# A graph layer with convolutions by frequency: gate weights summed one per batch, statistics in a row, weight transforms ahead of the first convolution, another order of tiles in the last phase, z behind n at the end

## The chip, the cores and the metric

One core of one Trainium2 chip. The metric is the device time of one execution in microseconds (us). The core has TensorE (PE; its weight loads PEld), VectorE (DVE), ScalarE (ACT), GpSimd (POOL) and SyncE (SP); SPq, ACTq and POOLq mark DMA issues on an engine's queue. A tile is a named buffer on the chip, PSUM the memory that TensorE writes to. A transfer is issued by one instruction and has landed when its data is there. The granted clock is the share of its full clock that TensorE had.

## The reference, cut to what matters

```python
h = relu(layernorm(x))                         # x: (32, 512, 256), 32 batches
# one layer on h; its result is added to x
c = relu(bn1(conv1(h)))                        # 1 tap
c = bn2(conv2(c))                              # 17 taps
x_conv = relu(c + h)
s = h @ w_se.T + b_se                          # 3 columns
A = exp(-dist(s, s)) * adj                     # (32, 512, 512), adj is 0 or 1
x_nmp = A @ relu(h @ w_msg.T + b_msg)
gi = concat(x_conv, x_nmp) @ w_ih.T ; gh = h @ w_hh.T
r = sigmoid(gi_r + gh_r) ; z = sigmoid(gi_z + gh_z)
n = tanh(gi_n + r * gh_n)
return x + (1 - z) * n + z * h
```

## The kernel before

The 17 tap convolution is a product over frequencies, the gates use a seven-product form of the 2 x 2 block product. So the program runs through these stages:

1. First stage, batches 0 to 15: layer norm, transpose, first convolution, transform to frequencies (tile `xf`), and beside it the transform of the convolution's weights (`pw`).
2. First nodes stage, batches 0 to 15: messages, adjacency, sums of messages, and the products over the frequencies (`py`).
3. Second stage, batches 16 to 31, without weight transforms. GpSimd forms the combined gate weights (`combine_weights`) in it.
4. Second nodes stage, batches 16 to 31.
5. Last phase, 16 pairs of batches: inverse transform (`inverse`), gates r, z, n, blend, transposes back, store.

The parts that the change and the argument touch:

```python
def statistics(b):
    ...
    for c in range(NC):                                   # NC = 4
        nc.vector.bn_stats(stats[:, c, :], X[b][:, c, :])
        nc.vector.bn_aggr(mv[:, c, :], stats[:, c, :])
    nc.vector.tensor_scalar(rstd, mv[:, :, 1], LN_EPS, None, op0=ALU.add)
    nc.gpsimd.tensor_tensor(rstd, rstd, minus_half[:, :NC], op=ALU.pow)
...
def load_adj(b):                                          # one buffer
    ADJ[b] = pools["nodes"].tile([P, N // 32, P], FP, tag="adj", name=f"adj_{b}", bufs=1)
    rows = adj[b].rearrange("(j r) (g m) -> g r j m", r=32, g=4)
    for g in range(4):
        nc.sync.dma_start(ADJ[b][32 * g : 32 * (g + 1)], rows[g])      # pieces of 128 floats
...
def combine_weights(k):                                   # called in three batches of stage 3
    w = pools["sums"].tile([P, DC, G], FP, tag="wraw", ...)
    nc.sync.dma_start(w, src...)
    ...
    for dst, a in ((Q1, a11), (Q2, a12), (Q4, a22)):
        nc.gpsimd.tensor_copy(t[:, dst], a)
    nc.gpsimd.tensor_tensor(t[:, Q5], a21, a22, op=ALU.add)
    ...                                                   # three more sums, then one store
...
def load_pair(p, queue=nc.sync):
    NP[p] = pools["ops"].tile([P, 7, N], FP, tag="np", ...)
    HP[p] = pools["ops"].tile([P, 8, N], FP, tag="hp", ...)
    ...                                                   # yt tiles in the loop behind them
...
with phase("late"), phase("sw"), phase("ops", bufs=2), phase("work"), tc.manual_schedule():
    sw = pools["sw"].tile([P, K3, 7, 3, P], FP, name="sw")
    load_pair(0, nc.gpsimd)
    load_combined(sw, 0, 2)                               # on GpSimd's queue, 4.1 MB in all
    load_combined(sw, 2, 7)
    inverse(0)
    ...
        gates_rz(p, terms, between)
        ...
        gate_n(p, terms, not more)                        # with blend and store of the last pair
```

## Time and profile before

| | before |
|---|---|
| median of 3 runs | 1972.78 us (1970.61 to 1972.83) |
| span of the profiled run | 1971.5 us |
| first stage, to the first `pm` matmul | 181.2 us |
| first nodes stage, to the first `phT` of batch 16 | 309.1 us |
| second stage, to the first `pm` of the second nodes stage | 138.0 us |
| second nodes stage, to its last `pm`, and from there to the inverse | 280.5 + 29.9 us |
| inverse of the first pair, to the first gate matmul | 15.2 us |
| rest of the last phase | 1017.7 us |

The stages are read off TensorE's timeline: each ends where the first matmul of the next one starts. The prediction below shows the page and the waits. Two places that it did not look at closely also belong here, so they stand here. The first is one batch of the first stage on VectorE (start in us, duration, engine, line, operation; in brackets the idle time before and what ended it):

```profile
65.66 0.69 DVE L221 COPY wst<-pw 80x512 f32<-80x512 f32 x1 [1.64 <-PE pw L214]
66.27 0.41 DVE L234 BATCH_NORM_STATS2 stats<-x 128x6 f32<-128x256 f32 x1
66.72 0.18 DVE L235 BATCH_NORM_AGGREGATE mv<-stats 128x2 f32<-128x6 f32 x1
...
68.52 0.17 DVE L238 TENSOR_SCALAR rstd<-mv 128x4 f32<-128x4 f32 x1
...
72.49 1.27 DVE L221 COPY wst<-pw 80x512 f32<-80x512 f32 x2
```

Four such pairs follow each other, so from the first statistic to the instruction that adds epsilon pass 2.25 us. Behind it come the additions and copies out of PSUM that TensorE needs. VectorE waits for TensorE only once in the batch, 1.64 us, and TensorE waits in the same batch for the copies out of PSUM:

```profile
73.75 1.89 PE L214 MATMUL pw<-w2p,taps 17*80 17x512 f32 x8 [0.28 <-ACT wst L223]
```

So here the two engines hand work to each other in a loop, and a share of busy time (in 45.8 to 75.6 us VectorE 79%, TensorE 97%) does not tell which of them sets the pace. TensorE's busy time holds waiting, too: eight such `pw` matmuls take 1.10 us at 70.00 and 1.89 us here.

The second place is the end of the second nodes stage, the last adjacency loads and their reader:

```profile
917.80 1.38 SPq L330 DMA_DIRECT2D adj<-in_adj_dram  x3
...
921.65 0.35 SPq L405 DMA_DIRECT2D nd<-nmp  x1
...
928.38 2.06 DVE L390 STREAM_TRANSPOSE at<-adj 128x512 f32<-128x512 f32 x2
```

The fourth load follows the store at 922.04 (0.43 us). The reader has no bracket: it did not wait. The loads of the last two batches took 3.2 to 5.6 us from issue to landing.

### The profile page before, as it was taken

Reading aid. Unit: us, or ns where it says so; the run is one execution under the profiler, and the core shown is the slowest. Engines: PE = TensorE matmul, PEld = TensorE weight load, DVE = VectorE, ACT = ScalarE, POOL = GpSimd, SP = SyncE. Lnnn points to the kernel's source line nnn. Section 1 sums busy time; section 2 is a strip of 40 time slices with the busy share of each in tenths; the row PEclk is TensorE's granted clock in tenths of the full one; section 3 lists DMA queues with packets and bytes.
Section 4 is the critical chain, followed back from the end, with each engine's and each line's share of the span. In section 5 each row is a group of like instructions: output and inputs, shape, how many; then the busy total and the mean of one; then the engine's idle time right before and its main releaser. Section 6 shows DMA issues by size and latency. Waiting matters only on the chain.

```text
span 1971.5 us, 21287 instructions
## 1 busy us (share of the span) xinstructions
PE 1916.8 (97%) x7328; PEld 1185.1 (60%) x7328; DVE 1131.3 (57%) x2191; ACT 545.2 (28%) x930; POOL 570.3 (29%) x564
## 2 busy tenths in 40 slices
PE   7999999999888999999899999999999999999997
PEld 5667676766777767775555545555455554555453
DVE  7776666665775665656155455544555355544555
ACT  3545332332234333332122212222122221222121
POOL 2231333333332344432613322132212322133211
PEclk9999999999899999999899999999999999999998
DMA  8997987776554788785812443134421443134401
GB/s 209 287 262 221 250 240 233 232 215 208 180 175 144 215 245 260 228 240 153 267 46 80 126 126 97 42 113 125 126 61 65 126 126 112 41 98 126 126 12 53
DMA packets 237055, 309.89 MB, mean 157 GB/s; under 512 B 14339, under 2 KB 187331, under 8 KB 236563
## 3 DMA queue, kind: packets, MB, share of 16 engines
q1 hardware_dynamic: 217715, 251.48, 44.3%
q0 software_dynamic: 7008, 25.17, 4.6%
q10 hardware_dynamic: 12224, 31.86, 4.6%
q8 instruction: 59, 0.97, 0.2%
q14 instruction: 49, 0.40, 0.1%
HBM read 201.57 MB, written 106.89 MB: 156 GB/s over the span
## 4 chain that ended last, share of the span: by engine, by line
PE 88%; DVE 5%; DMA 3%; issue 2%; POOL 1%; ACT 1%; SPq 0%; POOLq 0%; DVEq 0%; ACTq 0%
PE pg L490 29%; PE pn L490 14%; PE pn L399 11%; PE py L317 10%; PE pm L350 6%; PE pc L479 5%; PE pc L269 3%; PE px L284 2%; PE pd L385 2%; PE po L619 2%; PE pw L214 1%; DVE stats L234 1%; DMA wd<-wst 1%; PE phT L256 1%; DMA sw<-ws 1%
## 5 line engine op out<-in xcount | busy, mean ns | idle before, releaser
L490 PE MATMUL pg<-hp,sw 128*128 128x512 f32 x448 | 229.9, 595 | 0.3 <-DMA sw<-ws 0.3
L490 PE MATMUL pg<-np,sw 128*128 128x512 f32 x448 | 229.3, 593 | 0.0
L490 PE MATMUL pg<-cp,sw 128*128 128x512 f32 x448 | 228.7, 592 | 0.0
L399 PE MATMUL pn<-A,msg 128*128 128x512 f32 x512 | 225.5, 593 | 0.3 <-DVE A L391 0.3
L468 POOL TENSOR_TENSOR hp<-hp 128x512 f32<-128x512 f32 x64 | 80.6, 1270 | 460.1 <-DMA hp<-hd 393.2
L399 PEld LDWEIGHTS pn<-A,msg 128*128 128x128 f32 x512 | 96.9, 190 | 111.6 <-issue 108.2
L503 ACT ACTIVATE rz<-rz,brz 128x512 f32<-128x512 f32 x96 | 69.3, 722 | 298.7 <-DVE rz L507 298.7
L309 POOL TENSOR_TENSOR both<-xf 128x256 f32<-128x256 f32 x78 | 61.0, 782 | 309.6 <-PE py L317 273.7
L317 PE MATMUL py<-wt,both 128*128 128x256 f32 x624 | 150.4, 384 | 0.0
L490 PEld LDWEIGHTS pg<-np,sw 128*128 128x128 f32 x448 | 85.4, 191 | 107.7 <-issue 106.4
L490 PEld LDWEIGHTS pg<-cp,sw 128*128 128x128 f32 x448 | 85.2, 190 | 107.5 <-issue 107.2
L390 DVE STREAM_TRANSPOSE at<-adj 128x512 f32<-128x512 f32 x128 | 136.1, 1098 | 10.8 <-DMA adj<-in_adj_dram 7.8
L468 POOL TENSOR_TENSOR cp<-cp 128x512 f32<-128x512 f32 x64 | 80.5, 1268 | 210.6 <-ACT cp L484 209.3
L317 PEld LDWEIGHTS py<-wt,both 128*128 128x128 f32 x624 | 114.2, 190 | 43.9 <-issue 27.0
L490 PEld LDWEIGHTS pg<-hp,sw 128*128 128x128 f32 x448 | 82.9, 191 | 92.8 <-issue 89.5
L312 POOL TENSOR_TENSOR wsum<-wt 128x512 f32<-128x512 f32 x78 | 106.0, 1361 | 78.9 <-DMA wt<-wd 66.6
L269 PE MATMUL pc<-w,hT 128*128 128x256 f32 x512 | 127.6, 406 | 0.6 <-DVE hT L257 0.6
L479 PEld LDWEIGHTS pc<-back,yt 120*128 120x128 f32 x1024 | 119.5, 195 | 12.5 <-issue 7.7
L350 PE MATMUL pm<-wmsg,hT 128*128 128x259 f32 x512 | 125.6, 398 | 0.0
L479 PE MATMUL pc<-back,yt 120*128 120x80 f32 (+1 forms) x1024 | 119.2, 278 | 4.6 <-DMA yt<-yd 4.6
L350 PEld LDWEIGHTS pm<-wmsg,hT 128*128 128x128 f32 x512 | 122.3, 327 | 0.7
L490 PE MATMUL pn<-hp,sw 128*128 128x512 f32 x224 | 115.1, 595 | 0.0
(117 smaller groups left out, 2888.0 us busy)
## 6 DMA issues: line engine op xcount, KB each, us to landing
wt<-wd SPq DMA_DIRECT2D x160, 256.0 KB, 5.5
adj<-in_adj_dram SPq DMA_DIRECT2D x128, 256.0 KB, 5.1
yd<-y ACTq DMA_DIRECT2D x80, 384.0 KB, 5.6
yt<-yd SPq DMA_DIRECT2D x60, 480.0 KB, 9.4
wd<-wst SPq DMA_DIRECT2D x64, 320.0 KB, 5.2
x<-in_x_dram SPq DMA_DIRECT2D x38, 512.0 KB, 5.9
hd<-hT SPq DMA_DIRECT2D x32, 512.0 KB, 3.9
nd<-nmp SPq DMA_DIRECT2D x32, 512.0 KB, 3.2
```

The lines of the kernel that those rows point to most:

```text
L269: nc.tensor.matmul(p[:, j, :], HT[b][:, ic, c * P : (c + 1) * P], w1[:, ic, :], start=(ic == 0), stop=(ic == DC - 1))
L284: nc.tensor.matmul(p[:, j * 2 * L : (j + 1) * 2 * L], H1[b][:, c0 + j, ic * P : (ic + 1) * P], fwd, start=True, stop=True)
L309: nc.gpsimd.tensor_tensor(both[:, 0], re, im, op=ALU.add)
L312: nc.gpsimd.tensor_tensor(wsum, wr, wi, op=ALU.add)
L317: nc.tensor.matmul(dst, v[:, ic, :], w[:, ic, :], start=(ic == 0), stop=(ic == DC - 1))
L350: nc.tensor.matmul(p[:, : D + NS], chunk(HT[b][:, ic, :], c), wmsg[:, ic, :], start=(ic == 0), stop=(ic == DC - 1))
L390: nc.vector.transpose(at.rearrange("p (j k) -> p j k", k=32), ADJ[b].rearrange("p j (q c) -> p c j q", c=NC)[:, mc])
L399: nc.tensor.matmul(p, MSG[b][:, mc, dc * P : (dc + 1) * P], A[b][:, mc, :], start=(mc == 0), stop=(mc == NC - 1))
L468: nc.gpsimd.tensor_tensor(t[:, dst, :], t[:, a, :], t[:, b, :], op=sub)
L479: nc.tensor.matmul(bk[:, t0:t1], YT[p][j * W + w][:, oc * P : (oc + 1) * P], back[:, u0 : u0 + t1 - t0], start=(w == 0), stop=(w == W - 1) ...
L490: nc.tensor.matmul(bk, sw[:, k, q, o, :], terms[k][q], start=(first and i == 0), stop=(i == len(ks) - 1), skip_group_check=True)
L503: nc.scalar.activation(rz[:, g, j, :], src, AF.Sigmoid, bias=brz[:, g : g + 1], scale=1.0)
```

## The change

It means to take seven GpSimd instructions at a time out of the way of GpSimd's other work in the second stage, to shorten the statistics, to load less at the start and make the first weight transforms ahead of the first convolution, to let the first loads of the last phase start early by laying their tiles over memory that is free early, and to end with z, which needs less work behind its last matmul than n. The prediction numbers these five parts: 1 gate weights, 2 statistics, 3 first tiles of the last phase, 4 start, 5 z behind n. The core of the diff:

```diff
-    load_x(1)                                   # at the start
...
             nc.vector.bn_stats(stats[:, c, :], X[b][:, c, :])
+        for c in range(NC):
             nc.vector.bn_aggr(mv[:, c, :], stats[:, c, :])
...
-    def combine_weights(k):
...
+    def combine_weights():
+        steps = []
+        for k, src in enumerate((w_hhT, w_ihT[D:], w_ihT[:D])):
+            w, t = (pools["sums"].tile([P, n, 3, P], FP, tag=f"w{n}", name=f"w{n}_{k}") for n in (4, 7))
+            ...
+            for j in range(4):
+                nc.sync.dma_start(w[:, j], a[:, j // 2, j % 2])
+            ...                                  # four sums, one step each, no copies
+            steps[-1] = partial(self_and_store, steps[-1], k, stores)     # seven stores
...
     def load_pair(p, queue=nc.sync):
+        yt = [pools["ops"].tile([ROWS, W // 2, D], FP, tag="yt", ...) for k in range(4)]
+        HP[p] = pools["ops"].tile([P, 8, N], FP, tag="hp", name=f"hp_{p}")
         NP[p] = pools["ops"].tile([P, 7, N], FP, tag="np", name=f"np_{p}")
-        HP[p] = pools["ops"].tile([P, 8, N], FP, tag="hp", name=f"hp_{p}")
...
         if g == 0:                              # first weight transforms ahead of the first convolution
+            one, two = between(b0)
+            for step in one:
+                step()
             transpose_h(b0)
+            for step in two:
+                step()
...
-            load_taps(gen, 1, nc.sync)          # now loaded in batch 0's turn, on GpSimd's queue
...
-                    if b % 4 == 2 and b // 4 < K3:
-                        combine_weights(b // 4)
-                    return [], []
+                    return combine[b - 2 : b - 1] if b > 1 else [], []
...
+                gates_rz(p, terms, between, [0])                    # last pair: r
+                gate_n(p, terms, True)                              # n
+                gates_rz(p, terms, lambda i: None, [1], then)       # z, with blend and store
```

More of the change, by code (lines that the diff above doesn't have):

```diff
@@ L416, in gnn_layer, with self_and_store @@
     B11, B12, B21, B22 = range(4)
-    def combine_weights(k):
-        src = [w_hhT, w_ihT[D:], w_ihT[:D]][k]
-        w = pools["sums"].tile([P, DC, G], FP, tag="wraw", name=f"wraw_{k}")
-        nc.sync.dma_start(w, src.rearrange("(c p) o -> p c o", p=P))
-        w = w.rearrange("p c (g i o) -> p c g i o", i=2, o=P)
-        a11, a21, a12, a22 = w[:, 0, :, 0], w[:, 0, :, 1], w[:, 1, :, 0], w[:, 1, :, 1]
-        t = pools["sums"].tile([P, 7, 3, P], FP, tag="wsum7", name=f"wsum7_{k}")
-        for dst, a in ((Q1, a11), (Q2, a12), (Q4, a22)):
-            nc.gpsimd.tensor_copy(t[:, dst], a)
-        nc.gpsimd.tensor_tensor(t[:, Q5], a21, a22, op=ALU.add)
-        nc.gpsimd.tensor_tensor(t[:, Q6], t[:, Q5], a11, op=ALU.subtract)
-        nc.gpsimd.tensor_tensor(t[:, Q7], a11, a21, op=ALU.subtract)
-        nc.gpsimd.tensor_tensor(t[:, Q3], a12, t[:, Q6], op=ALU.subtract)
-        nc.sync.dma_start(WS[k], t)
+    def combine_weights():
+        steps = []
+        for k, src in enumerate((w_hhT, w_ihT[D:], w_ihT[:D])):
+            w, t = (pools["sums"].tile([P, n, 3, P], FP, tag=f"w{n}", name=f"w{n}_{k}") for n in (4, 7))
+            a = src.rearrange("(c p) (g i o) -> p c i g o", p=P, i=2, o=P)
+            for j in range(4):
+                nc.sync.dma_start(w[:, j], a[:, j // 2, j % 2])
+            a11, a21, a12, a22 = (w[:, j] for j in range(4))
+            for dst, x1, x2, op in ((Q5, a21, a22, ALU.add), (Q6, t[:, Q5], a11, ALU.subtract),
+                                    (Q7, a11, a21, ALU.subtract), (Q3, a12, t[:, Q6], ALU.subtract)):
+                steps.append(partial(nc.gpsimd.tensor_tensor, t[:, dst], x1, x2, op=op))
+            stores = [(Q1, a11), (Q2, a12), (Q4, a22)] + [(q, t[:, q]) for q in (Q5, Q6, Q7, Q3)]
+            steps[-1] = partial(self_and_store, steps[-1], k, stores)
+        return steps
+    def self_and_store(step, k, stores):
+        step()
+        for q, src in stores:
+            nc.sync.dma_start(WS[k][:, q], src)
     def load_combined(sw, q0, q1):
@@ L437, in load_pair @@
     def load_pair(p, queue=nc.sync):
+        yt = [pools["ops"].tile([ROWS, W // 2, D], FP, tag="yt", name=f"yt_{p}_{k}", bufs=5) for k in range(4)]
+        HP[p] = pools["ops"].tile([P, 8, N], FP, tag="hp", name=f"hp_{p}")
         NP[p] = pools["ops"].tile([P, 7, N], FP, tag="np", name=f"np_{p}")
-        HP[p] = pools["ops"].tile([P, 8, N], FP, tag="hp", name=f"hp_{p}")
         YT[p] = []
@@ L445, in load_pair @@
             for k in range(2):
-                t = pools["ops"].tile([ROWS, W // 2, D], FP, tag="yt", name=f"yt_{b}_{k}", bufs=5)
+                t = yt[2 * j + k]
                 w = w0 + k * (W // 2)
@@ L494, in temp, with gates_rz @@
         return pools["late"].tile([P, N], FP, tag=role, name=f"{role}_{name}", bufs=2)
-    def gates_rz(p, terms, between):
-        RZ[p] = rz = pools["late"].tile([P, 2 * DC, 2, N], FP, tag="rz", name=f"rz_{p}", bufs=1)
+    def gates_rz(p, terms, between, outs=range(2), then=lambda i, j: None):
+        if 0 in outs:
+            RZ[p] = pools["late"].tile([P, 2 * DC, 2, N], FP, tag="rz", name=f"rz_{p}", bufs=1)
+        rz = RZ[p]
         ks = range(K3)
@@ L508, in result @@
             sigmoid(dst, o, i, j)
-        for o in range(2):
+            then(i, j)
+        for o in outs:
             b1[o] = bank(f"pg1_{p}_{o}")
@@ L514, in gates_rz @@
             nc.scalar.copy(p1[o], b1[o])
-        for o in range(2):
+        for o in outs:
             b2[o] = bank(f"pg2_{p}_{o}")
@@ L519, in gates_rz @@
             nc.vector.tensor_add(u2[o], p1[o], b2[o])
-        for o in range(2):
+        for o in outs:
             into(b1[o], Q2, o, ks, terms, False)
             sigmoid(b1[o], o, 0, 0)
+            then(0, 0)
         between(0)
-        for o in range(2):
+        for o in outs:
             into(b2[o], Q7, o, ks, terms, False)
@@ L528, in gates_rz @@
         between(1)
-        for o in range(2):
+        for o in outs:
             b3[o] = bank(f"pg3_{p}_{o}")
@@ L532, in gates_rz @@
             result(b3[o], u3[o], o, 1, 1)
-        for o in range(2):
+        for o in outs:
             into(b2[o], Q4, o, ks, terms, False)
             result(b2[o], p1[o], o, 1, 0)
-        for o in range(2):
+        for o in outs:
             into(b3[o], Q3, o, ks, terms, False)
@@ L563, in closing @@
             nc.scalar.activation(n, n, AF.Tanh, bias=b_in[:, i : i + 1], scale=1.0)
-        def blend(i, j, engine=nc.vector):
-            n, d = nt[:, i, j, :], rz[:, i, j, :]
-            engine.tensor_tensor(d, HP[p][:, 2 * i + j, :], n, op=ALU.subtract)
-            engine.tensor_tensor(d, d, rz[:, DC + i, j, :], op=mul)
-            engine.tensor_tensor(n, n, d, op=add)
         x1 = [bank(f"pn1_{p}_{k}") for k in range(2)]
@@ L598, in gate_n, with blend @@
         closing(x3[1], 0, 1)
-        if last:
-            blend(0, 0, nc.gpsimd)
-            blend(1, 1, nc.gpsimd)
-            blend(1, 0)
-            finish(p, 0)
-            blend(0, 1)
-            finish(p, 1)
-        else:
-            for i, j in ((0, 0), (1, 1), (1, 0), (0, 1)):
-                blend(i, j)
+        for i, j in ((0, 0), (1, 1), (1, 0), (0, 1)):
+            nc.vector.tensor_sub(rz[:, i, j, :], HP[p][:, 2 * i + j, :], nt[:, i, j, :])
+            if not last:
+                blend(p, i, j)
+    def blend(p, i, j):
+        n, d = NT[p][:, i, j, :], RZ[p][:, i, j, :]
+        nc.vector.tensor_mul(d, d, RZ[p][:, DC + i, j, :])
+        nc.vector.tensor_add(n, n, d)
     def finish(p, j):
@@ L638, in first_part @@
         if g == 0:
+            one, two = between(b0)
+            for step in one:
+                step()
             transpose_h(b0)
+            for step in two:
+                step()
         statistics(b0 + 1)
@@ L654, in first_part @@
                 normalise(b + 2)
-            one, two = between(b - b0)
+            one, two = between(b - b0) if b > 0 else ([], [])
             if b > b0:
@@ L681, in gnn_layer @@
             load_taps(gen, 0, nc.sync)
-            load_taps(gen, 1, nc.sync)
             def between(b):
-                if b and b % 2 == 0 and b // 2 + 1 < QI // PI:
+                if b % 2 == 0 and b // 2 + 1 < QI // PI:
                     load_taps(gen, b // 2 + 1)
@@ L737, in gnn_layer @@
             with phase("first", "sums"):
+                combine = combine_weights()
                 def between(b):
-                    if b % 4 == 2 and b // 4 < K3:
-                        combine_weights(b // 4)
-                    return [], []
+                    return combine[b - 2 : b - 1] if b > 1 else [], []
                 xf = freq_tile(1)
@@ L773, in between, with then @@
                         sums(NP[p + 1], False)
-            gates_rz(p, terms, between)
             if more:
+                gates_rz(p, terms, between)
                 inverse(p + 1)
                 sums(CP[p + 1], False)
-            gate_n(p, terms, not more)
+                gate_n(p, terms, False)
+            else:
+                def then(i, j):
+                    blend(p, i, j)
+                    if i != j:
+                        finish(p, j)
+                gates_rz(p, terms, between, [0])
+                gate_n(p, terms, True)
+                gates_rz(p, terms, lambda i: None, [1], then)
 def kernel(**inputs):
```

## The prediction

> **What bounds the kernel now.** I read the page's engine table and slices first, then TensorE's waits, then the timeline at each place where TensorE stands still.
>
> ```profile
> PE 1916.8 (97%) x7328; PEld 1185.1 (60%) x7328; DVE 1131.3 (57%) x2191; ACT 545.2 (28%) x930; POOL 570.3 (29%) x564
> PE   7999999999888999999899999999999999999997
> PEclk9999999999899999999899999999999999999998
> ...
> PE 88%; DVE 5%; DMA 3%; issue 2%; POOL 1%; ACT 1%; SPq 0%; POOLq 0%; DVEq 0%; ACTq 0%
> ```
>
> TensorE is busy 1916.8 of 1971.5 us and is 88% of the chain that ended last. The change alters no matmul, so only the 55 us of idle time and the stretches at a lower granted clock can shrink. The waits tell where those 55 us are:
>
> ```profile
> PE phT L256 <- issue: 12.9, 3, 5.9
> PE po L619 <- DVE nt L570: 9.5, 2, 6.7
> PE row L158 <- DVE diag L157: 9.0, 1, 9.0
> PE pc L479 <- DMA yt<-yd: 4.6, 2, 2.6
> ```
>
> (what waited, total us, times, longest). That is four places: the second convolution stage, the end, the start, and the entry to the last phase. The steady part of the last phase has none. The "issue" label of the first line hides the cause; the timeline of one of its three stalls shows it:
>
> ```profile
> 517.26 0.17 DVE L238 TENSOR_SCALAR rstd<-mv 128x4 f32<-128x4 f32 x1
> 517.60 1.41 POOL L426 COPY wsum<-wraw 128x384 f32<-128x384 f32 x3 [5.49 <-DMA wraw<-in_w_hhT_dram]
> 521.94 0.99 POOL L430 TENSOR_TENSOR wsum<-wraw,wsum 128x384 f32<-128x384 f32 x1
> 523.69 1.05 POOL L239 TENSOR_TENSOR rstd<-rstd,minus_half 128x4 f32<-128x4 f32 x1
> 524.78 1.45 DVE L245 TENSOR_SCALAR x<-x,mv,rstd 128x256 f32<-128x256 f32 x4 [6.15 <-POOL rstd L239]
> 525.29 2.03 PE L256 MATMUL phT<-ident,x 128*128 128x128 f32 x8 [2.25 <-issue]
> 527.00:531.00 4.00, 4.00 (x14) 3.29 (x13) 0.42 (x1) 2.38 (x6) 0.00 (x0) 0.62 0.95 335
> ```
>
> VectorE had the variance at 517.4, but GpSimd raised it to -0.5 only at 523.7, because the seven weight sums stood in its queue. The last line is a window's row (busy of PE, PEld, DVE, ACT, POOL, then the granted clock): after the gap the clock falls to 0.62.
>
> **What the Trainium skill says.** "TensorE: Matmul & The Clock Gate", Part 1 (The HAM clock gate): an idle TensorE drops to half clock and returns after a few us of work. The trace agrees: 4 us at mostly 0.50 after a 2.25 us gap, so a stall costs its gap and about 2 us more. The same page, "Architectural detail", calls the queues of ScalarE, VectorE and GpSimd strict FIFO: the 6.15 us above is such a wait. "DMA: Bandwidth & Descriptors", "Queues, rings and completion order": each DMA engine takes turns between queues packet by packet, so an earlier bulk load slows a later urgent one. This trace has no clean case of it. "SBUF — State Buffer", "Who interferes with whom": a VectorE instruction with two SBUF inputs contends with GpSimd's reads. At the end L558 takes 1.64 us beside a GpSimd blend, against its 0.72 us mean.
>
> **The change part by part.**
>
> *1. Gate weights, one sum per batch.* Transforms of successive batches (L284) are 6.50 us apart when nothing stalls (507.69, 514.20, 520.70; also 583.25, 589.75). From 507.69 to 618.29 there are 13 steps in 110.6 us; 13 x 6.50 = 84.5. So the three bursts cost 26.1 us: steps of 11.3 and 8.4, 15.7 and 7.6, 14.0 and 8.0. Now GpSimd has 12 sums of 0.99 us, one each in batches 2 to 13, and no copies. The queue is free for 4.4 us between its pow and the next one, so a sum fits. It delays the next x load by 1 us, which has about 3 us in hand: issue to landing is 7.0 us in the median, and VectorE gains 0.4 us per batch from part 2.
>
> What it adds: the tiles have one buffer, so the second and third weight can be loaded only when the stores of the previous one have landed. The last sum of weight 0 comes in batch 5, the first of weight 1 in batch 6, 6.5 us later. In between lie seven stores (0.35 us of issue each, 1.4 MB), then four loads of 0.4 us issue, 512-byte pieces, 4 to 6 us to land: about 9 to 11 us. So that sum waits 2 to 5 us, the next x load behind it too, and x comes 0 to 2 us later than its slack allows. Twice 1.5 to 2 us, with a risk of a clock drop: -4. Net 22 us off.
>
> *2. Statistics in a row.* Four pairs of stats and aggregate take 2.23 us (4.67 to 6.90), each aggregate waiting for its stats. In a row, 256-element VectorE instructions start about 0.35 us apart (four L245 in 1.46), so 1.8 us. VectorE is not the bound except at the head of stage two, where a 3.8 us gap waits for x: 0.5 us off.
>
> *3. First tiles of the last phase over the frequencies.* The entry to the last phase:
>
> ```profile
> 933.90 0.79 POOL L448 DMA_DIRECT2D yt<-yd  x1 [21.22 <-DVE at L390]
> 944.96 1.12 PE L479 MATMUL pc<-back,yt 120*128 120x72 f32 x8 [2.60 <-DMA yt<-yd]
> 948.08 5.39 PE L479 MATMUL pc<-back,yt 120*128 120x80 f32 x24 [2.00 <-DMA yt<-yd]
> 953.81 2.05 PE L490 MATMUL pg<-hp,sw 128*128 128x512 f32 x2 [0.33 <-DMA sw<-ws]
> ...
> 925.00:935.00 10.00, 9.74 (x23) 3.98 (x22) 7.23 (x10) 1.40 (x3) 1.09 (x2) 1.00 0.02 5
> 945.00:955.00 10.00, 7.67 (x34) 6.63 (x34) 1.50 (x2) 1.42 (x2) 7.05 (x7) 0.57 1.04 358
> ```
>
> GpSimd's queue stands for 21.2 us on one yt load, whose tile lies over the adjacency that VectorE still reads; everything behind it, sw included, is late. The DMA engines carry 5 GB/s in 925 to 935, then 358 at full share. Adding tile sizes, sw starts at about 45 KB per partition and the tiles behind it at 77 KB; the frequencies end at about 121 KB. With yt (20 KB) and then hp in front, both lie over the frequencies, free at 908. So yt, hp, np and sw, 8.2 MB, go from 909 on: at 360 GB/s some 23 us, done near 938, when the inverse begins. That inverse takes 7.1 us elsewhere in the chain of waits, here 15.2 (938.63 to 953.81), and the gates behind it start at half clock until 956.6 (1.3 us lost): 9.4 us off. Against it: the last adjacency loads (917.8 to 922.0) now share the engines with the bulk load. VectorE needs them at 928.4 and they landed near 925; at a third to a half of the engines they land at 928 to 933. I take 3 us. Net 6.5 off.
>
> *4. Start.* The first weight transforms (16 matmuls, 2.8 us at 19.66) move in front of the first convolution. But TensorE there waits for VectorE's chain of statistics, and three PSUM copies of 0.69 us move into that chain too; statistics give 3 x 0.4 back. One x load and half the taps no longer crowd the first x. I take 0.5 off.
>
> *5. z behind n.* In the last pair r (18.0 us of matmuls), n (18.0), z (18.0). Before, 17.4 us pass from the last gate matmul (1954.1) to the end. Now behind the last z matmul come add 0.69, sigmoid 0.72, two VectorE steps 1.4 and waits, 3.2 us, then 5.4 to 6.0 us of transposes, additions and store (1965.53 to 1971.5 now): 9 us. Two gaps eat that. First, r alone reaches its fourth product 7.7 us after its start instead of 15.4, while VectorE is at the previous pair's blends until 1908.5: some 2.4 us. Second, the transposes of the pair's first batch stand in TensorE's program before the last z product and need its predecessor's sigmoid and blend: 3.5 us idle, then half clock for 1 us of transposes and 2.6 us of matmuls, about 2.5 us more, and the transposes themselves moved ahead. 9 + 2.4 + 3.5 + 2.5 + 1 = 18.4 against 17.4. Taking GpSimd out of the end speeds VectorE but not the new path. I take 0.5 us longer.
>
> Sum: 22 + 0.5 + 6.5 + 0.5 - 0.5 = 29 us off: **1943.8 us**.
>
> **Rivals.** (a) The single buffer takes the burst's place: the sum waits for its weight, x comes late, TensorE stalls at two batches with a clock drop each. For it: an x load already ends VectorE's idle time after each burst (3.7 us). Against it: part 2 gives VectorE room. Then part 1 yields only 14: about 1952. (b) The transfers collide: adjacency is 5 us late and the clock drops, so part 3 yields 2: 1948. With (a): 1956. (c) The gaps of part 5 are hidden or do not drop the clock, the adjacency arrives in time, the start gains 2 us: 26 + 0.5 + 9.4 + 2 + 3 = 41, 1932. For (c): adjacency loads ended VectorE's idle time in only 7.8 us of the whole run.
>
> **Range and chances.** (a) with (b) and (c) are the ends; each needs several steps to fall the same way, so 8 in 10 lie in 1934 to 1956. Faster by 2% needs 1934 or less, nearly all of (c): 0.09. Slower would need a new wait of 70 us, which nothing shows: 0.01.
>
> **What would show it right or wrong.** Step 1: transforms 6.5 us apart throughout, except perhaps near batches 6 and 10, where GpSimd waits on the weight load; wrong if longer steps remain elsewhere. Step 3: yt and sw issued near 910, the inverse in about 7 us, full clock in the first gate; wrong if VectorE then waits on adjacency for over 5 us. Step 4: the third batch's transposes near 24 us as now. Step 5: one gap of about 3.5 us before the last z product, one of 2 us in r; the end some 17 us behind the time at which the matmuls would have finished unbroken. Wrong altogether if the steady pair period of the last phase (62.98 us) moves.

## The result, and the profile after

| | before | after |
|---|---|---|
| median | 1972.8 us (6 runs) | 1963.89 us (1959.72 to 1964.9, 6 runs) |
| ratio | | 0.9946, 95% interval 0.9932 to 0.9961: the same within 2% |
| span of the profiled run | 1971.5 | 1962.5 |

Ratios are the mean time of one kernel's fast runs over that of the other's of the same rounds, so not quite the ratio of the medians.

The prediction said 29 us off, 1943.8 us, and 1934 to 1956 as the range. Measured were 9 us off, outside the range. Rows of the page that answer to those of before (the mean granted clock is 0.987 for 0.985):

```profile
PE 1903.5 (97%) x7328; PEld 1176.7 (60%) x7328; DVE 1129.6 (58%) x2197; ACT 545.5 (28%) x930; POOL 559.2 (28%) x554
...
PE   7999999999889999996999999999999999999997
...
PE 93%; DVE 2%; DMA 2%; issue 1%; SPq 1%; POOL 0%; ACT 0%; DVEq 0%; POOLq 0%
```

The 9 us look like a small gain everywhere. The stages show that they are large gains less a large loss:

| stage | before | after | gain |
|---|---|---|---|
| first stage | 181.2 | 176.5 | 4.7 |
| first nodes stage | 309.1 | 308.6 | 0.5 |
| second stage | 138.0 | 126.4 | 11.6 |
| second nodes stage, to its last `pm` | 280.5 | 280.5 | 0.0 |
| from there to the inverse | 29.9 | 47.8 | **-17.9** |
| inverse of the first pair | 15.2 | 7.1 | 8.1 |
| rest of the last phase | 1017.7 | 1015.7 | 2.0 |
| sum | | | 9.0 |

TensorE's waits name the loss (what waited, total us, times, longest):

```profile
PE pn L399 <- DVE A L391: 14.2, 1, 14.2
...
PE phT L256 <- issue: 8.1, 2, 4.2
PE po L623 <- DVE nt L612: 6.5, 3, 3.1
```

The first is new, and its timeline is that of the adjacency:

```profile
900.98 1.38 SPq L330 DMA_DIRECT2D adj<-in_adj_dram  x3
...
904.82 7.25 SPq L405 DMA_DIRECT2D nd<-nmp  x1
...
912.12 2.68 SPq L330 DMA_DIRECT2D adj<-in_adj_dram  x1
...
927.44 2.04 DVE L390 STREAM_TRANSPOSE at<-adj 128x512 f32<-128x512 f32 x2 [14.11 <-DMA adj<-in_adj_dram]
...
930.20 9.65 PE L399 MATMUL pn<-A,msg 128*128 128x512 f32 x16 [14.16 <-DVE A L391]
```

A store whose issue took 0.35 us now takes 7.25 us, the fourth load stands behind it, the loads land up to 23.2 us after issue, VectorE waits 14.11 us for them and TensorE 14.16 us for VectorE. The 16 matmuls behind the gap then take 9.65 us for the usual 7.1, and the 16 ahead of it take 8.83, with the clock at half for 3.4 us from 908.0. What else moved in 901 to 925 us is in the trace's queue rows for that window (packets, MB, share of the 16 DMA engines):

```profile
q0 software_dynamic: 1330, 6.44, 82.7%
q1 hardware_dynamic: 1778, 1.26, 21.8%
```

q0 carries the loads issued by GpSimd: the frequencies are free at 892, the bulk of the last phase (8.2 MB) starts there, and it is still running when the adjacency (1.05 MB) is issued on q1. The queues send similar numbers of packets, but a packet of q0 is 4.8 KB and one of q1 0.7 KB (6.44 MB over 1330 and 1.26 MB over 1778), so q1 gets 16% of the bytes. That fits turns taken by count and not by bytes. The Trainium skill, "DMA: Bandwidth & Descriptors", "Queues, rings and completion order", has each DMA engine go round the queues that have work for it, one packet at a time. Its packets are typically 9 to 17 descriptors, while the trace's seem to be single pieces (the mean of 0.7 KB on q1 is near the 512 bytes of an adjacency piece), so the window agrees with it but does not show the turns themselves.

The second stage has gained, but not all of its bursts' cost. GpSimd now waits at each change of weight (here at the second one):

```profile
573.03 0.61 SPq L437 DMA_DIRECT2D ws<-w  x1
...
576.78 0.99 POOL L668 TENSOR_TENSOR w<-w 128x384 f32<-128x384 f32 x1 [9.45 <-DMA hd<-hT]
...
580.78 2.33 PE L256 MATMUL phT<-ident,x 128*128 128x128 f32 x8 [4.20 <-issue]
```

The sum stands 9.45 us in GpSimd's queue with the pow of the statistics (variance to the power -0.5) behind it (at 578.52). (The bracket names the transfer that the profile saw last; a store of the previous weight was still being issued at 573.03, as the tile has one buffer.) At the head of that stage there is a new wait:

```profile
484.93 1.55 SPq L425 DMA_DIRECT2D w<-in_w_hhT_dram  x2
...
497.39 1.25 POOL L312 TENSOR_TENSOR wsum<-wt 128x512 f32<-128x512 f32 x1 [10.14 <-DMA wt<-wd]
498.61 1.03 POOL L239 TENSOR_TENSOR rstd<-rstd,minus_half 128x4 f32<-128x4 f32 x1
...
500.14 2.37 PE L256 MATMUL phT<-ident,x 128*128 128x128 f32 x8 [8.91 <-DVE x L245]
```

Four loads of raw gate weights went ahead of the last `wt` of the stage before (issued at 486.65 and 487.97). GpSimd's sum of that `wt` waits 10.14 us, and the pow, for which VectorE had its part done at 492.9, comes at 498.6. Before, that gap of TensorE was 3.81 us.

Last, the first stage. A batch's statistics are now 1.67 us from first to last (68.81 to 70.48, against 2.21 from 66.27 to 68.48):

```profile
68.81 1.39 DVE L233 BATCH_NORM_STATS2 stats<-x 128x6 f32<-128x256 f32 x4
70.12 0.36 DVE L235 BATCH_NORM_AGGREGATE mv<-stats 128x2 f32<-128x6 f32 x4
70.51 0.17 DVE L238 TENSOR_SCALAR rstd<-mv 128x4 f32<-128x4 f32 x1
```

And the batches follow each other 9.4 us apart where it was 9.9 (transposes at 49.5, 59.0, 68.1, 77.6; before at 45.8, 55.9, 65.5, 75.6), though the third batch starts 4.1 us later (28.3 against 24.2).

### The profile page after: what moved, and what is told of

Its sections match the earlier page's. It is cut to its first block, busy times and chain, and to the rows that moved or that the text cites. A ratio compares the mean times of both kernels' runs of the same rounds, so it can differ in the third digit from the quotient of the medians.

```text
span 1962.5 us, 21327 instructions
## 1 busy us (share of the span) xinstructions
PE 1903.5 (97%) x7328; PEld 1176.7 (60%) x7328; DVE 1129.6 (58%) x2197; ACT 545.5 (28%) x930; POOL 559.2 (28%) x554
## 4 chain that ended last, share of the span: by engine, by line
PE 93%; DVE 2%; DMA 2%; issue 1%; SPq 1%; POOL 0%; ACT 0%; DVEq 0%; POOLq 0%
PE pg L497 29%; PE pn L497 14%; PE pn L399 11%; PE py L317 10%; PE pm L350 6%; PE pc L486 6%; PE pc L269 5%; PE px L284 3%; PE pw L213 2%; PE pd L385 2%; PE phT L256 1%; PE po L623 1%; DMA adj<-in_adj_dram 1%; DMA wt<-wd 1%; PE psl L371 1%
## 5 line engine op out<-in xcount | busy, mean ns | idle before, releaser
L399 PE MATMUL pn<-A,msg 128*128 128x512 f32 x512 | 229.5, 602 | 14.2 <-DVE A L391 14.2
L390 DVE STREAM_TRANSPOSE at<-adj 128x512 f32<-128x512 f32 x128 | 135.9, 1095 | 26.0 <-DMA adj<-in_adj_dram 23.2
L269 PE MATMUL pc<-w,hT 128*128 128x256 f32 x512 | 122.9, 395 | 0.3 <-DVE hT L257 0.3
```

The source lines that it names most:

```text
L269: nc.tensor.matmul(p[:, j, :], HT[b][:, ic, c * P : (c + 1) * P], w1[:, ic, :], start=(ic == 0), stop=(ic == DC - 1))
L390: nc.vector.transpose(at.rearrange("p (j k) -> p j k", k=32), ADJ[b].rearrange("p j (q c) -> p c j q", c=NC)[:, mc])
L399: nc.tensor.matmul(p, MSG[b][:, mc, dc * P : (dc + 1) * P], A[b][:, mc, :], start=(mc == 0), stop=(mc == NC - 1))
```

## The experiments

Theory: (1) the bulk loads of the last phase starve the last adjacency loads, which costs 18 us and undoes part 3; (2) the single buffers and the early weight loads eat most of part 1; (3) the statistics in a row are worth some 9 us or more, as VectorE does set the pace in the first stage; (4) the new start costs 4 us. Each run stands against before, on the same chip; "against after" is the difference of its ratio and 0.9946, times 1972.8. Each of the two ratios is known to about 0.0015, so this difference is uncertain by some 4 us; the stages of the profiled runs are compared beside it. Those vary as well: in the runs that leave them as in after, the first stage ends at 173.9 to 176.5 us and the second takes 120.3 to 126.4. All results were correct.

| run | median us | ratio (95%) | against after, us |
|---|---|---|---|
| after | 1963.89 | 0.9946 (0.9932 to 0.9961) | |
| mem_back | 1955.3 | 0.9904 (0.9889 to 0.9919) | -8.3 |
| sw_act | 1965.14 | 0.9948 (0.9935 to 0.9960) | +0.4 |
| nd_act | 1965.36 | 0.9954 (0.9941 to 0.9966) | +1.6 |
| sums2 | 1952.04 | 0.9881 (0.9867 to 0.9894) | -12.8 |
| sw_last | 1956.09 | 0.9919 (0.9906 to 0.9933) | -5.3 |
| adj2 | 1948.18 | 0.9884 (0.9869 to 0.9899) | -12.2 |
| w_late | 1954.15 | 0.9908 (0.9894 to 0.9921) | -7.5 |
| stats_only (on before) | 1959.14 | 0.9935 (0.9923 to 0.9948) | |
| start_back | 1956.69 | 0.9920 (0.9907 to 0.9934) | -5.1 |
| stats_twice | 1983.75 | 1.0059 (1.0046 to 1.0071) | +22.3 |
| best1 | 1929.65 | 0.9785 (0.9772 to 0.9799) | -31.8 |
| best3 | 1925.51 | 0.9762 (0.9749 to 0.9775) | -36.3 |

### The loss at the end of the second nodes stage

**mem_back**: part 3 undone alone.

```diff
     def load_pair(p, queue=nc.sync):
-        yt = [...]; HP[p] = ...; NP[p] = ...     # yt and hp first
+        NP[p] = ...; HP[p] = ...                 # np, hp, and yt in the loop, as before
```

> The changed kernel with only the old order of tiles in the last phase (part 3 undone). Theory 1 (the bulk loads of the last phase, now free to start at 892 us, take the DMA engines from the last adjacency loads): the 14 us TensorE wait on A before the last pn vanishes, the time from the last pm to the inverse falls from 47.8 to about 30 us, the entry to the gates grows back from 7 to about 15 us; together about 8 to 10 us faster than the changed kernel's 1963.9, so 1955 (ratio to before 0.990 to 0.991). Rival (the wait has another cause, such as the order of the queue after the earlier second stage): the wait stays, only the entry gets slower, 1972.

Measured: the wait on A is gone, the part to the inverse is 29.9 us again, the inverse 14.5 us. The kernel is 8.3 us faster without part 3. Theory 1 holds as to the part; what of it costs is the next question.

**sw_act**: half of the bulk on ScalarE's queue.

```diff
-            nc.gpsimd.dma_start(sw[:, k, q0:q1], WS[k][:, q0:q1])
+            nc.scalar.dma_start(sw[:, k, q0:q1], WS[k][:, q0:q1])
```

> The changed kernel with the 4.1 MB of combined weights loaded from ScalarE's queue, so behind its last exponentials (about 930 us), and only yt, hp and np (4.1 MB) early. Theory 1: those are done by about 905, the last adjacency loads find free engines, TensorE's wait on A falls from 14 to under 3 us, and the combined weights land by about 942, in time for the gates: 12 to 18 us faster than the changed kernel, 1946 to 1952 (ratio 0.987 to 0.990). If the weights are too late for the first gate, the entry grows from 7 to 10 us or so. Rival (the wait has another cause): 1964, wait of 14 us unchanged.

A miss of the experiment, not of the theory: the build does not keep program order between the nodes stage and the last phase, so the six loads were issued at 891.8 to 899.9 on ScalarE's queue, no later than before. The wait on A was 15.8 us, the time unchanged. It shows that for this half of the bulk the issuing queue did not matter, as it came at the same time.

**nd_act**: the store that stood between the adjacency loads, moved away.

```diff
-        nc.sync.dma_start(ND[b], NMP.pop(b))
+        (nc.sync if b < GB else nc.scalar).dma_start(ND[b], NMP.pop(b))
```

> The changed kernel with the stores of the messages' sums in the second nodes stage issued from ScalarE's queue, so the adjacency loads no longer stand behind a store that took 7.25 us to issue. Theory 1 (engines shared): the bulk still shares the engines, adjacency still lands in 10 us or more, TensorE's wait stays at 7 us or more, time 1957 to 1964. Rival 2 (only the queue's order: the fourth adjacency load was issued 7 us late behind the store): the wait falls from 14 to about 5 us or less, time 1952 to 1955.

The last four adjacency loads now stand together, and still:

```profile
901.78 11.29 SPq L330 DMA_DIRECT2D adj<-in_adj_dram  x4
```

In before four such loads took about 1.8 us to issue. TensorE's wait on A was 19.0 us. Rival 2 (only the queue's order) falls: with the store gone, the loads' own issue is what takes long, and they land up to 28.2 us after it. Theory 1 stays; the time is 1.4 us above its range, within the noise.

**sw_last**: the weights' tile laid over the adjacency, so that its load must wait for the end of the stage.

```diff
-    with phase("late"), phase("sw"), phase("ops", bufs=2), phase("work"), tc.manual_schedule():
+    with phase("late"), phase("ops", bufs=2), phase("sw"), phase("work"), tc.manual_schedule():
```

> The changed kernel with the pool of the combined weights laid behind the other tiles of the last phase, so over the adjacency and the messages: its 4.1 MB can only be loaded when the last sums of messages have read those (about 930), while yt, hp and np (4.1 MB) still go early. This does what the run with ScalarE's queue was meant to do and did not (there the loads were issued at 892 to 900, as early as before). Theory 1 (the bulk shares the engines with the adjacency): TensorE's wait on A falls from 14 to under 4 us, the part from the last pm to the inverse from 47.8 to 31 to 36 us; the first two of seven weights land before the first gate, the entry stays below 9 us: 10 to 15 us faster than the changed kernel, 1949 to 1954 (ratio 0.987 to 0.990). Rival A (the weights then come too late): the first gates wait 3 to 6 us for sw, 1955 to 1959. Rival B (half of the bulk is enough to delay the adjacency): wait of over 8 us remains, 1960 to 1964.

With half of the bulk out of the way the wait on A fell from 14.2 to 4.4 us and the part to the inverse from 47.8 to 37.1. But the weights now come late, and GpSimd, which issues them, starts its own sums later (a first gate matmul also waits 0.79 us for a weight at 937.1):

```profile
928.86 3.21 POOL L441 DMA_DIRECT2D sw<-ws  x6 [31.88 <-PE pn L399]
...
945.03 1.12 PE L497 MATMUL pg<-cp,sw 128*128 128x512 f32 x2 [1.25 <-POOL cp L475]
```

From the first gate to the end it is 3.6 us longer than after (1019.3 against 1015.7). Theory 1 and rival A both, 1956.09 in all.

**adj2**: the adjacency a batch earlier, the bulk untouched.

```diff
-        ADJ[b] = pools["nodes"].tile([P, N // 32, P], FP, tag="adj", name=f"adj_{b}", bufs=1)
+        ADJ[b] = pools["nodes"].tile([P, N // 32, P], FP, tag="adj", name=f"adj_{b}", bufs=2)
...                                              # and one buffer instead of two for sl
```

> The changed kernel with two buffers for the adjacency (and one instead of two for sl, to make room), so that the last adjacency can be loaded some 10 us earlier, before the bulk of the last phase. The bulk itself is not touched. Theory 1 (the late adjacency is all that costs): the wait on A falls from 14 us to under 3 us, and the part from the last pm to the inverse from 47.8 to 30 to 34 us: 13 to 17 us faster than the changed kernel, 1947 to 1951 (ratio 0.986 to 0.988). Rival (other transfers shared with the bulk, such as the stores, delay the end too): 1955 to 1960.

The last four loads were issued at 879.7, ahead of the bulk, and the last 32 matmuls of the stage ran without a break, at full clock:

```profile
906.57 14.00 PE L399 MATMUL pn<-A,msg 128*128 128x512 f32 x32
```

The part to the inverse is 29.1 us, 18.7 less. The bulk runs as before this edit, so its other transfers cost nothing: the late adjacency was all of the loss. The time fell by 12.2 us, less than 18.7. One reason is that two adjacencies now go ahead of `wt` at the head of the first nodes stage (TensorE waits 3.6 us there, that stage is 5.7 us longer than after); best1 below takes two buffers in the second nodes stage alone. The account is not exact: the profiled spans differ by 17.0 us, as the second stage, which the edit leaves alone, was 6.1 us shorter in this run.

### The second stage

**sums2**: two buffers.

```diff
-            w, t = (pools["sums"].tile([P, n, 3, P], FP, tag=f"w{n}", name=f"w{n}_{k}") for n in (4, 7))
+            w, t = (pools["sums"].tile([P, n, 3, P], FP, tag=f"w{n}", name=f"w{n}_{k}", bufs=2) for n in (4, 7))
```

> The changed kernel with two buffers for the raw weight and for its sums. Theory 2 (single buffer: GpSimd's sum waits 8.5 and 9.5 us for the next weight, x late behind it): both waits vanish, transforms stay 6.5 us apart through all batches, the two longer steps (8.5 and 14.2 us for 6.5) go: 9 to 10 us faster than the changed kernel, 1954 to 1955 (ratio 0.990 to 0.991). Rival (the sums themselves in GpSimd's queue, or VectorE's order, make the steps long): the long steps stay, 1962 to 1964. The stall at the entry, from weight loads in front of the last wt, stays or grows by up to 3 us, as eight loads instead of four may stand there.

The transforms are 6.5 us apart in all batches and both waits are gone, as expected of theory 2. The stage is 15.6 us shorter (110.8 for 126.4), more than the 9 to 10 expected, because the wait at its head fell too: TensorE's third transposes waited 3.3 us (3.81 in before). Eight loads stood in front of `wt` there, and it landed later; but that moved GpSimd's sum of it from ahead of the pow to behind it. So a later load cost less. This part of the expectation was wrong.

**w_late**: one buffer, but each raw weight loaded where the program stands.

```diff
-            for j in range(4):                  # all three ahead of the stage
-                nc.sync.dma_start(w[:, j], a[:, j // 2, j % 2])
+        def load(k): ...                        # the same four loads
+        def step(b):
+            if b == 1:
+                load(0)
+            ...                                 # the sum of batch b; after the fourth sum seven stores and load(k + 1)
```

> The changed kernel with each raw weight loaded where the program of the stage stands: the first in the second batch's turn instead of ahead of the stage, still with one buffer. Theory (weight loads in front of the last wt on SyncE's queue hold GpSimd's sum of wt, and with it the pow and the third batch, 5 us more than before): the 8.9 us stall at the stage's third transpose falls to about 4 us, the two stalls at the change of weights stay at 8 to 10 us together: 4 to 6 us faster than the changed kernel, 1958 to 1960 (ratio 0.992 to 0.993). Rival (the entry stall comes from x or from GpSimd alone): it stays, 1963 to 1964. The single buffered stalls could also grow by a few us, as the order of loads and stores is now that of the program.

At the head of the stage the loads of `wt` are first again, GpSimd's sum waits 1.47 us instead of 10.14, and TensorE's third transposes 3.26 us instead of 8.91:

```profile
483.15 0.90 SPq L296 DMA_DIRECT2D wt<-wd  x2
...
487.40 1.26 POOL L312 TENSOR_TENSOR wsum<-wt 128x512 f32<-128x512 f32 x1 [1.47 <-DMA wt<-wd]
```

The stage took 117.0 us, 9.4 less: 5.6 at the head, and the longer steps at the changes of weights were 7.6 and 11.6 us for 8.5 and 14.2. The second part was not expected. It is not clearly the edit's: the later of the two steps is 11.3 to 14.2 us long in the runs whose second stage is as in after.

### The first stage

**stats_only**: part 2 alone, on the kernel before.

```diff
             nc.vector.bn_stats(stats[:, c, :], X[b][:, c, :])
+        for c in range(NC):
             nc.vector.bn_aggr(mv[:, c, :], stats[:, c, :])
```

> The kernel before with the statistics in a row, nothing else. The prediction gave 0.5 us for it. The trace of the changed kernel suggests that each batch of the first convolution stage is 0.6 us shorter (14 batches, about 8 us), as VectorE is nearly the bound there: 6 to 9 us faster than before, ratio 0.9955 to 0.997. If the prediction's step was right: ratio 0.9995 to 1.0.

One line alone gives as much as all five parts together: ratio 0.9935 against 0.9946, and more than the 6 to 9 us expected. The first stage is 171.2 us (10.0 less), the second 133.1 (4.9 less). Step 2 of the prediction (0.5 us) is wrong by a factor of over 20. Of the 10.0 us, 16 batches times 0.54 us are 8.6. The rest may be the clock: the stage had half clock for 3.4 us three times in before and twice here, which I estimate at 1.7 us. How much of the 4.9 us is the statistics' is not shown: they lie mostly in the steps of the bursts, and such steps vary between runs (11.3 to 14.2 us for one of them, above).

**stats_twice**: the reverse, on the changed kernel (same result).

```diff
+        if b < GB:
+            for c in range(NC):
+                nc.vector.bn_stats(stats[:, c, :], X[b][:, c, :])
         for c in range(NC):
             nc.vector.bn_aggr(mv[:, c, :], stats[:, c, :])
```

> The changed kernel with each batch's four statistics instructions of the first convolution stage made twice (same result, 1.3 us of VectorE per batch more). It asks whether VectorE's length counts there, which the prediction denied. If VectorE's chain bounds the batch with nearly no slack left: 16 batches become 0.7 to 1.3 us longer each, the stage's end moves from 176.5 to 187 to 197 us, and the time to 1974 to 1984 (ratio 0.9995 to 1.0045). If VectorE has slack there and the gain came from elsewhere (the first transforms, clock): the end of the stage stays within 3 us, 1963 to 1966.

The four extra instructions take 1.3 us, the batches are now 10.8 us apart instead of 9.4 (transposes at 53.7, 64.5, 75.2, 86.0), and the stage ends at 195.8, 19.3 later. So nearly every us of VectorE's statistics is a us of the first stage. Rival (slack) falls. Three batches each of before, after and this run, as rows of windows (stretch, its length, busy us of PE, PEld, DVE, ACT and POOL, granted clock, share of the DMA engines, GB/s):

```profile
45.80:75.60 29.80, 29.05 (x171) 20.41 (x169) 23.64 (x60) 15.17 (x35) 8.30 (x11) 1.00 1.01 286
49.50:77.60 28.10, 28.10 (x171) 20.34 (x169) 22.41 (x60) 15.10 (x35) 8.25 (x11) 1.00 0.99 301
53.70:86.00 32.30, 30.32 (x170) 20.80 (x169) 26.32 (x72) 14.82 (x34) 8.25 (x11) 1.00 0.92 265
```

The clock is full in all three, so it is not the cause here. In after TensorE is recorded as busy 100% and VectorE 80%, and still VectorE's time counts. For the same matmuls TensorE's busy time is 28.10 to 30.32 us, so part of it is waiting.

**start_back**: part 4 undone alone.

```diff
     load_x(0)
+    load_x(1)
...
             load_taps(gen, 0, nc.sync)
+            load_taps(gen, 1, nc.sync)
...                                              # and the weight transforms behind the first convolution again
```

> The changed kernel with the start as before (second x and second half of the taps loaded at once, the first weight transforms behind the first convolution). The trace shows the third batch's transposes at 28.3 us instead of 24.2; the run with the statistics alone has them at 23.7 and ends the first stage at 171.2 instead of 174 to 176.5. Theory: the new start costs 4 us: the first stage ends at 171 to 172.5, 3 to 5 us faster than the changed kernel, ratio 0.992 to 0.993. If the prediction was right (0.5 us gained by the new start): no faster, 0.9945.

The third batch's transposes are at 24.3 again, the stage ends at 171.5, and the kernel is 5.1 us faster than after. Part 4 costs 2 to 5 us, given where the first stage ended in the runs that keep it (173.9 to 176.5). Which of its edits costs how much was not tried apart. In after the first statistics start at 6.22 us and the first convolution at 18.25, here at 4.63 and 12.71; in between stand the weight transforms and their copies.

### Together

**best1**: start_back, two buffers for the raw weights and sums with each load in the program's turn, and two adjacency buffers in the second nodes stage.

```diff
+        ADJ[b] = ...tile(..., tag="adj", bufs=1 if b < GB else 2)        # and sl with one buffer
+        ...                                     # w_late with bufs=2 and load(k + 1) behind the second sum
+    load_x(1)                                   # and the rest of start_back
```

> All the mends together on the changed kernel: old start (4 us), two buffers for raw weights and sums with each weight loaded in the program's turn (15 to 17 us), two buffers for the adjacency in the second nodes stage only (17 to 18 us there, without the 5 us that two buffers cost at the entry to the first nodes stage). Theory: they are independent, since they lie in four stages: 36 to 39 us off 1963.9, so 1925 to 1928 (ratio 0.976 to 0.978). If they share a bound (engine sharing moves to another transfer): 1932 to 1940.

Against after the profiled span is 37.1 us shorter (1925.4), of which 5.9 lie in the first stage, 16.2 in the second, 17.0 before the inverse; 2.3 are given back at the head of the second nodes stage, where a load of h comes late. The ratios say 31.8, a little under the 36 to 39 expected of independent parts (the uncertainty is some 4 us).

**best3**: and the transposes of the last pair's first batch behind the last z product.

```diff
                 def then(i, j):
+                    if (i, j) == (0, 1):
+                        finish(p, 0)
                     blend(p, i, j)
-                    if i != j:
-                        finish(p, j)
+                    if (i, j) == (0, 1):
+                        finish(p, 1)
```

> As best1, with the transposes of the last pair's first batch moved behind the last z product in TensorE's program. In the changed kernel TensorE waits 3.1 us for them ahead of that product and then again 3.0 us at the end. Theory: the first wait goes and the end is 2 to 4 us shorter than best1's. Rival: VectorE and ScalarE, not TensorE, carry the end; then less than 1 us.

The wait ahead of the last z product in the changed kernel, and that of the same transposes here:

```profile
1950.55 0.98 PE L623 MATMUL po<-ident,nt 128*128 128x128 f32 x7 [3.11 <-DVE nt L612]
```

```profile
1915.38 0.98 PE L631 MATMUL po<-ident,nt 128*128 128x128 f32 x7 [0.53 <-DVE nt L620]
```

The wait behind it, for the second batch's blend, went from 2.99 to 2.27 us. From the first gate to the end it is 1012.1 us against best1's 1015.4: 3.3 less, inside the 2 to 4. In sum 1925.51 us, ratio 0.9762: faster than both kernels. TensorE's share of the span is now 99%:

```profile
PE 1895.9 (99%) x7328; PEld 1174.5 (61%) x7328; DVE 1126.1 (59%) x2197; ACT 545.6 (28%) x930; POOL 553.8 (29%) x549
```

## Why the prediction was wrong

Nearly all that moved moved where the prediction looked; the wait for `wt` at the head of the second stage was not in it. Four of its five sizes were wrong, and the errors partly cancelled (some 36 us too much for steps 1, 3 and 4, some 15 too little for steps 2 and 5): that the sum was off by 20 us and not by more is luck.

| step | predicted gain | measured | from |
|---|---|---|---|
| 1 gate weights | 22 | 6.7 | second stage, stats_only 133.1 to after 126.4 |
| 2 statistics | 0.5 | 14.9 | stages of stats_only, 10.0 + 4.9 |
| 3 first tiles | 6.5 | -8.3 | mem_back; by stages 8.1 + 1.5 - 17.9 |
| 4 start | 0.5 | -5.0 | start_back, 171.5 against 176.5 (2 to 5 over the runs) |
| 5 z behind n | -0.5 | +0.5 | last pair's r to the end, 73.3 to 72.8 |
| sum | 29 | 8.8 | measured in all: 9.0 |

The rows of steps 1 and 2 divide the second stage's gain by the order in which the parts were added; that division is not sharp, as said at stats_only.

**Step 1.** The mechanism is right: the bursts cost 26.1 us, and with the two mends (two buffers, loads in their turn) the second stage of best1 is 110.2 us, 22.9 less than that of stats_only. The wrong term is "Twice 1.5 to 2 us, with a risk of a clock drop: -4". The sums waited 8.5 and 9.5 us, not 2 to 5, because a store and the loads of the next weight follow each other on SyncE's queue between other work; the long steps cost 9.7 us. The prediction also overlooked that the first weight's loads go ahead of the last `wt`, 5.1 us at the head. Its rival (a) named the first of the two, and its sign to look for (longer steps near batches 6 and 10) was there.

**Step 2.** The step that failed: "VectorE is not the bound except at the head of stage two". The saving per batch was worked out well (0.43 us; measured 0.54). But the batches of the first stage pass it on nearly one for one, 10.0 us there, and the second stage of stats_only was 4.9 us shorter too. The prediction read TensorE's 97% and a VectorE that was often idle as slack. In this loop TensorE was recorded as busy 97 to 100% and VectorE as 79 to 80%, and VectorE's time counted all the same.

**Step 3.** The gain was right: inverse in 7.1 us, no half clock behind it, 8.1 + 1.5 = 9.6 for the predicted 9.4. The step that failed: "at a third to a half of the engines they land at 928 to 933. I take 3 us". The adjacency got 16% of the bytes, and its loads were held already at their issue; 14.2 us of wait and slower matmuls on both sides of it made 17.9. Rival (b) had the mechanism, with 5 us late instead of 14, and the sign "wrong if VectorE then waits on adjacency for over 5 us" is what the trace showed. The predicted range ended at 1956, with (a) and (b) at the sizes given there. (Two sums of this step are slightly off: 909 and 23 us give 932, not 938, and 9.4 less 3 is 6.4.)

**Step 4.** "I take 0.5 off" was a guess about a chain that the prediction had described: weight transforms and copies ahead of the first convolution. The step that failed is the balance of that chain, in which shorter statistics and fewer early loads were to pay for it: the first convolution starts 5.5 us later than in start_back. Its sign (third batch near 24 us) failed with 28.3.

**Step 5.** Right within 1 us: gaps of 3.11 us before the last z product and 1.67 us in r, against 3.5 and 2 predicted. That the sum fits is in part luck, for the half clock came at the other gap. The windows of the six gate matmuls behind each, the gap in r first:

```profile
1900.70:1905.10 4.40, 4.38 (x7) 1.79 (x8) 1.16 (x2) 0.14 (x1) 0.00 (x0) 0.61 0.34 119
1951.30:1954.10 2.80, 2.80 (x9) 1.02 (x6) 1.12 (x2) 0.00 (x0) 0.00 (x0) 1.00 0.51 180
```

Behind the gap in r they ran at a clock of 0.61 and took 4.5 us for 2.7; behind the predicted one at full clock.

## What to carry to other kernels

When a change lets a bulk transfer start earlier, list the small urgent loads that will then be in flight beside it, do not take for granted that each queue gets an even share of the bytes, and load them ahead. When engines hand work to each other in a loop, take 1 us of the less busy one out or put 1 us in before calling it slack; busy time can hold waiting. Extra loads on a queue delayed what stood behind them at the seam of two stages; try issuing them in the turn of the batch that uses them.

## What the Trainium skill lacked or had wrong

- "DMA: Bandwidth & Descriptors", "Queues, rings and completion order", states the turns by packet, but not what two queues with different packets then get: here 0.7 KB beside 4.8 KB got 16% of the bytes, and loads that took 3.2 to 5.6 us took up to 23.2.
- "Perfetto Trace Analysis", "DMA Instruction — HWDGE (DVE, Sync)", does not say how long an issue can stand while other transfers fill the DMA engines: beside the bulk a store's issue went from 0.35 to 7.25 us, and four adjacency loads together took 11.29 us, so everything behind on that queue came late too. That the full engines held it is the likely cause, not tested apart.
- "VectorE: DVE Perf Modes", "The DRAIN you can't avoid", says that chaining without semaphores gains nothing, and does not speak of the order of dependent operations. Here the same eight operations took 2.21 us as four dependent pairs and 1.67 us with the four statistics first, and that order was worth some 12 us of the kernel (stats_only).
- "TensorE: Matmul & The Clock Gate", Part 1, gives about 3.4 us of idle time for the drop to half clock. Here 3.4 us at half clock followed gaps of 2.25 us (before, from 526.6) and of 1.67 us (after, from 1901.3), while the gap of 3.11 us in after had none right behind it and the same gap in adj2 (3.10 us) had. So the length of the gap alone did not decide.
